# Biases, own features and residual sums: from TensorE and ScalarE to VectorE in a four-layer graph network kernel

## The chip, the cores and the metric

The kernel runs on one core of a Trainium2 chip. Its time is the device time of one execution in microseconds (us). The engines are named as the profile names them: PE (TensorE matmul), PEld (TensorE weight load), DVE (VectorE), ACT (ScalarE), POOL (GpSimd), SP (SyncE). They run their own queues of instructions side by side and wait for one another by semaphores. Line numbers such as L812 are those of the kernel before.

## What is computed

Sixteen graphs (batches) of 1024 nodes with 64 features each go through four layers, each followed by a layer norm of the sum of its input and its output. Layer 0 multiplies by the adjacency matrix and applies an MLP with tanh. Layer 1 is a mean over the neighbours, weighted by the adjacency. Layers 2 and 3 take, for each node and each feature, a weighted sum of three quantiles over the node's neighbours, after some edges are removed ("dilation"), add the node's own features, and apply an MLP with relu.

```python
def _L0(h, adjacency, W1, b1, W2, b2):
    messages = jnp.einsum('bij,bjh->bih', adjacency, h)
    node_in = jnp.concatenate([h, messages], axis=-1)
    return jnp.tanh(node_in @ W1 + b1) @ W2 + b2

def _L1(x, A):
    deg = jnp.clip(jnp.sum(A, axis=2, keepdims=True), 1.0, None)
    return jnp.matmul(A / deg, x)

def _L2(x, adj, mask, W1, b1, W2, b2):          # _L3 is the same in form
    adj_d = _dilate_adj(adj, mask)
    agg = _weighted_nanquantile_agg(x, adj_d > 0)   # quantiles 0.25, 0.5, 0.75
    out = (1.0 + EPS_GIN) * x + agg
    h = jax.nn.relu(jnp.einsum('bnc,ch->bnh', out, W1) + b1)
    y = jnp.einsum('bnh,ho->bno', h, W2) + b2
    return y * mask[..., None].astype(dtp)

x = _layernorm(x + _L0(x, adj, ...))
x = _layernorm(x + _L1(x, adj))
x = _layernorm(x + _L2(x, adj, nodemask, ...))
x = _layernorm(x + _L3(x, adj, nodemask, ...))
```

## The kernel before

The nodes of a graph are 8 tiles of 128 (NT = 8); two halves of four tiles (NH = 2, G = 4) are handled at a time. The nodes are sorted by the number of their neighbours, so that each tile has lists of one length. Seven tiles get their neighbours' features by indirect DMA (`got_s`), the eighth, with up to 33 slots, by matmuls with one-hot matrices: VectorE makes `hot` for a slot, TensorE picks the rows into `pgk`, ScalarE copies four slots at a time. VectorE then sorts the lists with networks of min and max.

The parts of all graphs are written as Python generators and woven together when the program is built. Each `yield n` says that the generator's next instructions are to be placed n us of VectorE work later in the source; the count is kept as VectorE's instructions are issued (`Metered`). A `yield` costs no time on the chip: it only sets the order of the instructions in each engine's queue. Round k sorts layer 2 of graph k and layer 3 of graph k - 2.

```python
    # features(b, e): layers 0 and 1 of a graph
        for h in range(NH):
            ...
            pd = s.psum.tile([P, G, C], F32, name="pd", tag="x", bufs=1)
            for q in range(G):
                nc.tensor.matmul(pd[:, q, :], hid_t[:, q * P : (q + 1) * P], w02s, start=True, stop=False)
                nc.tensor.matmul(pd[:, q, :], ones_row, bias_rows[0], start=False, stop=False)
                nc.tensor.matmul(pd[:, q, :], ident, x_s[:, h * G + q, :], start=False, stop=True)
            yield 10
            nc.scalar.copy(y[:, h * G : (h + 1) * G], pd)                       # L451
        yield 4
        yield from settle(x1[:, :, :C], y, "x")                                 # layer norm
        ...
            dve.tensor_scalar(deg[:, 0], pa[:, :, C], 1.0, None, op0=ALU.max)
            dve.reciprocal(deg[:, 1], deg[:, 0])
            yield 1
            for q in range(G):
                nc.scalar.activation(y[:, h * G + q, :], pa[:, q, :C], AF.Copy, scale=deg[:, 1, q : q + 1])  # L475

    # lists(b, e, pace): the neighbours' numbers and counts (cut)
            yield 2.6
        yield 3
        dve.tensor_scalar(own[:, :, 0], key[:, 4], 1.0, None, op0=ALU.add)
        ...
    # ordered(b, e, order, own): each entry's slot number (cut)
            for c in range(g, g + G):
                for c2 in range(c + 1):
                    nc.tensor.matmul(pp[:, c - g, :], steps[:, ONSET + (c - c2) * P :][:, :P], place[:, c2, :], ...)
            yield 9
            dve.tensor_mul(place[:, g : g + G, :], pp, place[:, g : g + G, :])

    # fill(k): the long tile's slots (cut)
            for i in range(1, size):
                ...
                hot = s.lists.tile([P, NT, P], BF, name="hot", bufs=HOTS)       # HOTS = 6
                dve.tensor_scalar(hot, e.place, float(i), None, op0=ALU.is_equal)
                ...
                pick(pg[:, i - first, :], hot, e.parts[m], whole)               # 24 matmuls
                yield 2.1

    # finish(b, e, layer, agg): own features, MLP, mask, layer norm
        for h in range(NH):
            pt = s.psum.tile([P, HALF], F32, name="pt", tag="m", bufs=1)
            for q in range(G):
                nc.tensor.matmul(pt[:C, q * P : (q + 1) * P], xc[:, h * G + q, :], ident, start=True, stop=False)
                nc.tensor.matmul(pt[:C, q * P : (q + 1) * P], agg[:, h * G + q, :], ident, start=False, stop=True)
            yield 7
            nc.scalar.copy(o_t, pt[:C])
            yield 3
            nc.tensor.matmul(ph[:H], w1s, o_t, start=True, stop=True)
            yield 7
            nc.scalar.activation(h_t, ph[:H], AF.Relu, bias=b1c)
            yield 3
            pd = s.psum.tile([P, G, C], F32, name="pd", tag="m", bufs=1)
            for q in range(G):
                nc.tensor.matmul(pd[:, q, :], h_t[:, q * P : (q + 1) * P], w2s, start=True, stop=False)
                nc.tensor.matmul(pd[:, q, :], ones_row, bias_rows[1 + layer], start=False, stop=True)
            yield 9
            for t in range(h * G, (h + 1) * G):
                nc.scalar.activation(y[:, t, :], pd[:, t - h * G, :], AF.Copy, scale=e.mask[:, t : t + 1])   # L812
        yield 4
        dve.tensor_add(y, y, xc)
        yield from settle(xn, y, "m")
```

Of the kernel before, what the change touches and what calls it, by code (L numbers as in the profile page):

```python
# [21 lines left out]
P = 128  # L22
# [190 lines left out]
def adj_resnorm_kernel(ctx: ExitStack, tc: tile.TileContext, x, adj_t, nodemask, w01, b01, w02, b02,  # L213
# [53 lines left out]
        nc.sync.dma_start(t, ap)  # L267
        return t

    def row(ap, name):  # L270
        return weight(ap.rearrange("(o c) -> o c", o=1), name)

    def column(ap, name):
        return weight(ap.rearrange("(c o) -> c o", o=1), name)

    w01s, b01c, w02s = weight(w01, "w01s"), column(b01, "b01c"), weight(w02, "w02s")
    mlps = [
        (weight(w21, "w21s"), column(b21, "b21c"), weight(w22, "w22s")),
        (weight(w31, "w31s"), column(b31, "b31c"), weight(w32, "w32s")),
    ]  # L280
    bias_rows = [row(b, f"bias_row{i}") for i, b in enumerate((b02, b22, b32))]
    ones_row = const.tile([1, P], F32, name="ones_row")
    nc.vector.memset(ones_row, 1.0)
    def hats(dst, pos_shape, n1, places):

        m = s.work.tile(pos_shape, F32, name="hat_m", tag=f"hat_m{pos_shape[-1]}", bufs=1)
# [116 lines left out]
    def features(b, e):  # L403

        x_s = s.feat.tile([P, NT, C], F32, name="x_s", bufs=1)
        load_x(b, x_s)
        adj = {}

        def load(i):

            if i < 2 * NT:
                adj[i] = s.feat.tile([P, NT, P], F32, name="adj_r", bufs=3)
                cols = slice(i % NT * P, i % NT * P + P)
                nc.sync.dma_start(adj[i], adj_t[entry(b), :, cols].rearrange("o (t p) i -> p (o t) i", p=P))

        load(0)
        load(1)
        x1 = s.feat.tile([P, NT, C + 1], F32, name="x1", bufs=1)
        y = s.work.tile([P, NT, C], F32, name="y_x", bufs=1)
        dve.memset(x1[:, :, C : C + 1], 1.0)  # L420
        yield 8
        for h in range(NH):

            node_in = s.work.tile([P, HALF], F32, name="node_in", bufs=1)
            px = s.psum.tile([P, HALF], F32, name="px", tag="x", bufs=1)
            for q in range(G):
# [12 lines left out]
            yield 3  # L439
            nc.tensor.matmul(px[:C], w01s, node_in, start=True, stop=True)  # L440
            yield 9
            hid_t = s.work.tile([C, HALF], F32, name="hid_t", tag="node_in", bufs=1)
            nc.scalar.activation(hid_t, px[:C], AF.Tanh, bias=b01c)
            yield 3
            pd = s.psum.tile([P, G, C], F32, name="pd", tag="x", bufs=1)
            for q in range(G):
                nc.tensor.matmul(pd[:, q, :], hid_t[:, q * P : (q + 1) * P], w02s, start=True, stop=False)
                nc.tensor.matmul(pd[:, q, :], ones_row, bias_rows[0], start=False, stop=False)
                nc.tensor.matmul(pd[:, q, :], ident, x_s[:, h * G + q, :], start=False, stop=True)
            yield 10  # L450
            nc.scalar.copy(y[:, h * G : (h + 1) * G], pd)  # L451
        yield 4
        yield from settle(x1[:, :, :C], y, "x")
        while b and not entries[b - 1].packed:
            yield 2
        near = s.sets.tile([P, NT, N], F16, name="near")
        for h in range(NH):
            pa = s.psum.tile([P, G, C + 1], F32, name="pa", tag="x", bufs=1)
            for q in range(G):
                i = NT + h * G + q  # L460
                t = i - NT
                rows = slice(t * P, (t + 1) * P)
                for jt in range(NT):
                    nc.tensor.matmul(pa[:, q, :], adj[i][:, jt, :], x1[:, jt, :], start=jt == 0, stop=jt == NT - 1)  # L464
                yield 4
                dve.tensor_scalar(near[:, :, rows], adj[i], 0.0, None, op0=ALU.is_gt)
                dve.tensor_mul(near[:, t, rows], near[:, t, rows], off_diag)
                load(i + 2)
            yield 8
            deg = s.work.tile([P, 2, G], F32, name="deg", bufs=1)  # L470
            dve.tensor_scalar(deg[:, 0], pa[:, :, C], 1.0, None, op0=ALU.max)
            dve.reciprocal(deg[:, 1], deg[:, 0])
            yield 1
            for q in range(G):
                nc.scalar.activation(y[:, h * G + q, :], pa[:, q, :C], AF.Copy, scale=deg[:, 1, q : q + 1])  # L475
        yield 5
        e.near = near
        x2 = s.feat.tile([P, NT, C], F32, name="x2", tag="x_s", bufs=1)
        dve.tensor_add(y, y, x1[:, :, :C])
        yield from settle(x2, y, "x")  # L480
        nc.sync.dma_start(table[0][b % 3][:N, :].rearrange("(t p) c -> p t c", p=P), x2)
        while b >= 2 and not entries[b - 2].filled[0]:
            yield 2
        parts = s.feat.tile([P, NT, 3, C], BF, name="x2p")
        yield from split(x2, parts, y)
        e.parts[0] = parts

    def lists(b, e, pace):
# [69 lines left out]
        for t in range(NT + 1):  # L558
# [12 lines left out]
                junk = s.work.tile([P, NT, P], F16, name="junk", tag="dist", bufs=3)  # L571
                nc.scalar.activation(junk, left(t - 1), AF.Sign, accum_out=key[:, 4, t - 1 : t])
            yield 2.6
        yield 3


        dve.tensor_scalar(own[:, :, 0], key[:, 4], 1.0, None, op0=ALU.add)
# [57 lines left out]
    def ordered(b, e, order, own):  # L635
# [41 lines left out]
        for g in reversed(range(0, NT, G)):  # L677
            pp = s.psum.tile([P, G, P], F32, name="pp", tag="s", bufs=1)
            for c in range(g, g + G):
                for c2 in range(c + 1):  # L680
                    nc.tensor.matmul(pp[:, c - g, :], steps[:, ONSET + (c - c2) * P :][:, :P], place[:, c2, :],
                                     start=c2 == 0, stop=c2 == c)
            yield 9
            dve.tensor_mul(place[:, g : g + G, :], pp, place[:, g : g + G, :])
            yield 3
        e.place = place
# [43 lines left out]
    def fill(k):  # L730
# [6 lines left out]
        for m, b, e in members(k):  # L737
# [8 lines left out]
            for i in range(1, size):  # L746
# [6 lines left out]
                    nc.tensor.matmul(pg[:, i - first, :], e.none,  # L753
                                     ident_b[: KW - 1, i - 1 : i].to_broadcast([KW - 1, C]), start=True, stop=False)
                pick(pg[:, i - first, :], hot, e.parts[m], whole)
                yield 2.1
                if i % 4 == 2 and waiting:
                    empty()
                if i % 4 == 0:
# [26 lines left out]
    def finish(b, e, layer, agg):  # L786

        xc = e.xs[layer]
        w1s, b1c, w2s = mlps[layer]
        y = s.work.tile([P, NT, C], F32, name="y_m", bufs=1)  # L790
        for h in range(NH):
            pt = s.psum.tile([P, HALF], F32, name="pt", tag="m", bufs=1)
            for q in range(G):
                nc.tensor.matmul(pt[:C, q * P : (q + 1) * P], xc[:, h * G + q, :], ident, start=True, stop=False)
                nc.tensor.matmul(pt[:C, q * P : (q + 1) * P], agg[:, h * G + q, :], ident, start=False, stop=True)
            yield 7
            o_t = s.work.tile([C, HALF], F32, name="o_t", bufs=1)
            nc.scalar.copy(o_t, pt[:C])
# [6 lines left out]
            yield 3  # L805
            pd = s.psum.tile([P, G, C], F32, name="pd", tag="m", bufs=1)
            for q in range(G):
                nc.tensor.matmul(pd[:, q, :], h_t[:, q * P : (q + 1) * P], w2s, start=True, stop=False)
                nc.tensor.matmul(pd[:, q, :], ones_row, bias_rows[1 + layer], start=False, stop=True)
            yield 9  # L810
            for t in range(h * G, (h + 1) * G):
                nc.scalar.activation(y[:, t, :], pd[:, t - h * G, :], AF.Copy, scale=e.mask[:, t : t + 1])  # L812
        yield 4
        dve.tensor_add(y, y, xc)
        xn = agg if layer else s.feat.tile([P, NT, C], F32, name="x3s", bufs=3)
        yield from settle(xn, y, "m")
# [175 lines left out]
        nc.vector.reciprocal(st[:, 0], st[:, 3])  # L992
        nc.vector.tensor_mul(dst, y, st[:, 0, :, None].to_broadcast([P, NT, C]))

    def per_row(ap):
        t = s.work.tile([P, C], F32, name="per_row")
        nc.sync.dma_start(t, ap.rearrange("(o c) -> o c", o=1).to_broadcast([P, C]))
        return t

    def transposed(src, name):  # L1000

        dst = s.work.tile([C, N], F32, name=name, bufs=1)
# [7 lines left out]
    def layer0(adj_half, x_s, x1):  # L1010
# [18 lines left out]
            nc.tensor.matmul(pd[:, t, :], hid_t[:, t * P : (t + 1) * P], w02s, start=True, stop=True)  # L1029
        y = s.work.tile([P, NT, C], F32, name="y")  # L1030
        nc.vector.tensor_add(y, pd, x_s)
        nc.vector.tensor_add(y, y, per_row(b02)[:, None, :].to_broadcast([P, NT, C]))
        nc.vector.memset(x1[:, :, C : C + 1], 1.0)
        layernorm(x1[:, :, :C], y)

# [15 lines left out]
        nc.vector.tensor_add(y, y, x1[:, :, :C])  # L1051
        layernorm(x2, y)

    def mlp(xc, agg, mask, layer, dst):
        w1s, b1c, w2s = mlps[layer]
        y = s.work.tile([P, NT, C], F32, name="y")
        nc.vector.tensor_add(agg, agg, xc)
        o_t = transposed(agg, "x_t")
# [9 lines left out]
        nc.vector.tensor_add(y, pd, per_row((b22, b32)[layer])[:, None, :].to_broadcast([P, NT, C]))  # L1068
# [131 lines left out]
    with tc.If(nc.values_load(over_d[:, B:]) > 0):  # L1200
        with tc.For_i(0, B) as b:
            with tc.If(nc.values_load(over_d[:, ds(b, 1)]) > 0), ExitStack() as general:
# [32 lines left out]
                for layer, (xc, xn) in enumerate(((x2, x3), (x3, x1[:, :, :C]))):  # L1235
                    with tc.tile_pool(name=f"g_lists{layer}", bufs=1) as lists:
                        long_quantiles(lists, table[layer][0], idx, wts, agg)
                    with tc.tile_pool(name=f"g_dense{layer}", bufs=1) as dense:
                        dense_quantiles(dense, xc, valid, count, longest, agg)
                    mlp(xc, agg, mask, layer, xn)  # L1240
# [34 lines left out]
```

## Time and profile before

| | |
|---|---|
| time, median of 3 runs | 5381.86 us (5374.81 to 5388.84) |
| span of the profiled execution | 5376.9 us |
| mean granted TensorE clock | 0.765 of full speed |
| sixteen graphs, rounds | 18 rounds, some 316 us each in the steady part |

The page gives each engine's busy time as a share of the span, and the same in 40 slices as tenths. A wait is put down to the instruction that ended it. VectorE's instructions all stand at one line, L207 (the helper that counts them), so they are told apart by the tiles that they write and read. The largest groups that the change touches or has beside it are these (count, busy us, mean ns of one):

| engine | what | count | busy us | mean ns |
|---|---|---|---|---|
| PE | picks of the long tile, pgk<-x2p,hot and pgk<-x3p,hot | 24576 | 971.8 | 201 to 204 |
| PE | MLP bias, pd<-bias_row,ones_row (L809) | 512 | 133.0 | 347 |
| PE | features bias (L448) and own features (L449) | 512 | 142.3 | 363 and 375 |
| PE | transpose with sum, pt (L794 and L795) | 1024 | 253.4 | 333 to 348 |
| DVE | hot<-place 128x1024 | 1024 | 436.5 | 437 |
| ACT | mask, y_m<-pd,mask_s (L812) | 256 | 59.1 | 320 |
| ACT | degree scaling, y_x<-pa,deg (L475) | 128 | 29.3 | 309 |
| ACT | copy y_x<-pd (L451) | 32 | 12.0 | 376 |

### The profile page before, as it was taken

What the parts mean: (1) busy time and instruction counts of PE and PEld (TensorE: products, weight loads), DVE (VectorE), ACT (ScalarE), POOL (GpSimd) and SP (SyncE); (2) the same over time, 40 slices, a digit from 0 to 9 for tenths busy, and PEclk for the clock granted to TensorE, in tenths of its full rate; (3) what the DMA queues carried; (4) which work ended last, traced back from release to release, by engine and by line L of the source; (5) the groups of instructions that cost most, each with busy time, mean ns of one, the idle gap of its engine ahead of it and who ended that gap; (6) DMA issues with size and microseconds to landing.
All of it is one profiled execution on the core that took longest, in us unless ns stands there. A gap on an engine that the chain in (4) does not pass through costs nothing. (4 is left out here: it accounts for less than half of the span.)

```text
span 5376.9 us, 112554 instructions
## 1 busy us (share of the span) xinstructions
PE 3746.3 (70%) x45268; PEld 2875.6 (53%) x45304; DVE 4444.1 (83%) x8819; ACT 2296.3 (43%) x6214; POOL 3659.3 (68%) x3228
## 2 busy tenths in 40 slices
PE   6888876595967769595876849688694966434452
PEld 5656655374746657363655636466473745433341
DVE  2487777989898898979889797988979789977975
ACT  3364462455445363634445353443535344222222
POOL 0335575878777777867768686776868577777662
PEclk7887787696878779787877868687797877666655
DMA  2222321222222212112221221222122121111010
GB/s 82 64 60 54 79 49 50 50 51 61 53 60 54 58 48 65 41 35 59 56 56 46 48 52 42 60 55 54 41 56 53 40 46 24 25 23 25 19 24 10
DMA packets 420186, 259.37 MB, mean 48 GB/s; under 512 B 106164, under 2 KB 368452, under 8 KB 419652
## 3 DMA queue, kind: packets, MB, share of 16 engines
q0 software_dynamic: 102400, 105.06, 10.1%
q1 hardware_dynamic: 317252, 147.02, 9.8%
q8 instruction: 356, 5.83, 0.5%
q14 instruction: 178, 1.46, 0.1%
HBM read 239.27 MB, written 12.58 MB: 47 GB/s over the span
## 5 line engine op out<-in xcount | busy, mean ns | idle before, releaser
L359 POOL DMA_INDIRECT got_s<-table,idx x2944 | 3355.2, 1140 | 1473.6 <-issue 686.4
L355 PEld LDWEIGHTS <-hot 128*128 128x128 bf16 x24576 | 881.8, 104 | 611.8 <-DVE hot L207 468.2
L522 PE MATMUL pr<-steps,near 128*128 128x512 bf16 x1500 | 435.1, 453 | 378.0 <-ACT nb_st L503 223.8
L355 PE MATMUL pgk<-x3p,hot 128*128 128x64 bf16 x12288 | 493.2, 204 | 229.0 <-DVE hot L207 203.0
L355 PE MATMUL pgk<-x2p,hot 128*128 128x64 bf16 x12288 | 478.6, 201 | 239.1 <-DVE hot L207 216.1
L744 ACT COPY got<-pgk 128x256 f32<-128x256 f32 x256 | 94.5, 369 | 1186.0 <-PE pgk L355 1175.5
L207 DVE TENSOR_TENSOR other<-got_s 128x512 f32<-128x512 f32 (+8 forms) x900 | 514.8, 584 | 90.3 <-DMA got_s<-table,idx 75.5
L207 DVE TENSOR_SCALAR hot<-place 128x1024 bf16<-128x1024 f16 x1024 | 436.5, 437 | 129.8 <-PE pgk L355 127.2
L522 PEld LDWEIGHTS <-near 128*128 128x128 f16 x1536 | 171.2, 112 | 634.8 <-issue 521.1
L207 DVE TENSOR_TENSOR got_s<-got_s 128x384 f32<-128x384 f32 (+7 forms) x918 | 490.7, 537 | 17.5
L774 ACT ACTIVATE got_s<-got_s,wts 128x64 f32<-128x64 f32 x1568 | 400.2, 338 | 221.6 <-DVE got_s L207 221.0
L609 PE MATMUL pk<-near,order 128*128 128x512 f16 x2048 | 485.2, 393 | 0.0
L464 PE MATMUL pa<-x,adj_r 128*128 128x65 f32 x2048 | 355.2, 349 | 93.4 <-DMA adj_r<-in_adj_dram 39.2
L566 PE MATMUL pv<-minus_n,takes 128*128 128x128 bf16 x1024 | 224.7, 249 | 279.0 <-DVE takes L207 278.4
L207 DVE TENSOR_TENSOR got_s<-other 128x512 f32<-128x512 f32 (+8 forms) x774 | 409.2, 541 | 8.1
L464 PEld LDWEIGHTS pa<-x,adj_r 128*128 128x128 f32 x2048 | 343.4, 264 | 107.6 <-DMA adj_r<-in_adj_dram 40.5
L566 PEld LDWEIGHTS <-takes 128*128 128x128 bf16 x1024 | 112.9, 110 | 416.7 <-DVE takes L207 318.1
L207 DVE TENSOR_TENSOR other<-other 128x128 f32<-128x128 f32 (+13 forms) x558 | 318.6, 571 | 15.1
L609 PEld LDWEIGHTS <-order 128*128 128x128 bf16 x2048 | 198.5, 101 | 242.9 <-issue 42.5
L565 PE MATMUL pv<-scaled,near 128*128 128x128 f16 x1024 | 226.2, 250 | 105.0 <-ACT near L570 93.8
L528 ACT ACTIVATE junk<-pr,nb_st 128x1024 f16<-128x1024 f32 x256 | 282.1, 1107 | 28.7 <-PE pr L522 28.6
L431 PE MATMUL px<-adj_r,x_s 128*64 128x128 f32 x2048 | 274.7, 293 | 2.1 <-ACT node_in L434 1.4
(204 smaller groups left out, 7486.6 us busy)
## 6 DMA issues: line engine op xcount, KB each, us to landing
adj_r<-in_adj_dram SPq DMA_DIRECT2D x256, 512.0 KB
got_s<-table,idx POOLq DMA_INDIRECT x2944
x_s<-in_x_dram SPq DMA_DIRECT2D x16, 256.0 KB
table<-x SPq DMA_DIRECT2D x16, 256.0 KB
x<-table SPq DMA_DIRECT2D x16, 256.0 KB
table<-x3s,rows POOLq DMA_INDIRECT x128
out_dram<-agg,out_rows POOLq DMA_INDIRECT x128
table<-no_row SPq DMA_DIRECT2D x6, 0.2 KB
```

Of the source, the lines that this page charges most:

```text
L207: return call(*args, **kwargs)
L355: nc.tensor.matmul(dst, hot[:, c, :], parts[:, c, q, :], start=first and c + q == 0, stop=c == NT - 1 and q == 2)
L359: nc.gpsimd.indirect_dma_start(out=dst, out_offset=None, in_=tab, in_offset=bass.IndirectOffsetOnAxis(ap=rows, axis=0))
L431: nc.tensor.matmul(px[C:, q * P : (q + 1) * P], x_s[:, jt, :], adj[t][:, jt, :], start=jt == 0, stop=jt == NT - 1)
L464: nc.tensor.matmul(pa[:, q, :], adj[i][:, jt, :], x1[:, jt, :], start=jt == 0, stop=jt == NT - 1)
L522: nc.tensor.matmul(pr[:, h * HALF : (h + 1) * HALF], near[:, c, t * P : (t + 1) * P], steps[:, ONSET + h * HALF - c * P :][:, :HALF], star ...
L528: nc.scalar.activation(junk, prs[t - 1], AF.Sign, bias=lim[:, i, t - 1 : t], scale=-1.0, accum_out=cut_at[:, i, t - 1 : t])
L565: nc.tensor.matmul(pv[:, cols], near[:, c, rows], scaled[:, c, :], start=True, stop=False)
L566: nc.tensor.matmul(pv[:, cols], takes[:, c, rows], minus_n, start=False, stop=False)
L609: nc.tensor.matmul(cols, order[:, c, t * P : (t + 1) * P], left(c, slice(h * G, (h + 1) * G)), start=c == 0, stop=c == NT - 1)
L744: nc.scalar.copy(got[:, m, waiting[0] : waiting[0] + 4, :], waiting[1])
L774: nc.scalar.activation(prods[:, m, i, :], got[:, m, slot_id, :], AF.Copy, scale=e.wts[:, t, i : i + 1])
```

## The change

The change takes three kinds of addition out of TensorE's accumulation in PSUM, and two scalings out of ScalarE, and gives all of them to VectorE. The bias rows are loaded once, spread over the 128 partitions. It is to relieve TensorE and ScalarE, and to let VectorE read PSUM without another engine between. It also changes three distances in the source: the long tile's slots (2.1 to 2.4), the product that makes the slot numbers (`place`, 9 to 12), and the read-out of the counts (3 to 6).

```diff
-    def row(ap, name):
-        return weight(ap.rearrange("(o c) -> o c", o=1), name)
+    def per_row(ap, name):
+        t = const.tile([P, C], F32, name=name)
+        nc.sync.dma_start(t, ap.rearrange("(o c) -> o c", o=1).to_broadcast([P, C]))
+        return t
 ... (the weights of the layers now hold b02r, b22r, b32r; ones_row and bias_rows are gone)
@@ features
-                nc.tensor.matmul(pd[:, q, :], hid_t[:, q * P : (q + 1) * P], w02s, start=True, stop=False)
-                nc.tensor.matmul(pd[:, q, :], ones_row, bias_rows[0], start=False, stop=False)
-                nc.tensor.matmul(pd[:, q, :], ident, x_s[:, h * G + q, :], start=False, stop=True)
+                nc.tensor.matmul(pd[:, q, :], hid_t[:, q * P : (q + 1) * P], w02s, start=True, stop=True)
             yield 10
-            nc.scalar.copy(y[:, h * G : (h + 1) * G], pd)
-        yield 4
+            dve.tensor_add(y[:, h * G : (h + 1) * G], pd, x_s[:, h * G : (h + 1) * G])
+        dve.tensor_add(y, y, b02r[:, None, :].to_broadcast([P, NT, C]))
 ...
-            yield 1
-            for q in range(G):
-                nc.scalar.activation(y[:, h * G + q, :], pa[:, q, :C], AF.Copy, scale=deg[:, 1, q : q + 1])
-        yield 5
+            dve.tensor_mul(y[:, h * G : (h + 1) * G], pa[:, :, :C], deg[:, 1, :, None].to_broadcast([P, G, C]))
@@ lists
-        yield 3
+        yield 6
@@ ordered
-            yield 9
+            yield 12
             dve.tensor_mul(place[:, g : g + G, :], pp, place[:, g : g + G, :])
@@ fill
-                yield 2.1
+                yield 2.4
@@ finish
+        dve.tensor_add(agg, agg, xc)
+        yield 2
 ...
-                nc.tensor.matmul(pt[:C, q * P : (q + 1) * P], xc[:, h * G + q, :], ident, start=True, stop=False)
-                nc.tensor.matmul(pt[:C, q * P : (q + 1) * P], agg[:, h * G + q, :], ident, start=False, stop=True)
+                nc.tensor.transpose(pt[:C, q * P : (q + 1) * P], agg[:, h * G + q, :], ident)
 ...
-                nc.tensor.matmul(pd[:, q, :], h_t[:, q * P : (q + 1) * P], w2s, start=True, stop=False)
-                nc.tensor.matmul(pd[:, q, :], ones_row, bias_rows[1 + layer], start=False, stop=True)
+                nc.tensor.matmul(pd[:, q, :], h_t[:, q * P : (q + 1) * P], w2s, start=True, stop=True)
             yield 9
-            for t in range(h * G, (h + 1) * G):
-                nc.scalar.activation(y[:, t, :], pd[:, t - h * G, :], AF.Copy, scale=e.mask[:, t : t + 1])
-        yield 4
+            dve.tensor_add(y[:, h * G : (h + 1) * G], pd, b2r[:, None, :].to_broadcast([P, G, C]))
+        dve.tensor_mul(y, y, e.mask[:, :, None].to_broadcast([P, NT, C]))
         dve.tensor_add(y, y, xc)
```

What is cut away from the diff is in a path for graphs with longer lists, which these inputs do not take.

More of the change, by code (lines that the diff above doesn't have):

```diff
@@ L268, in weight @@
         return t
-    def row(ap, name):
-        return weight(ap.rearrange("(o c) -> o c", o=1), name)
+    def per_row(ap, name):
+        t = const.tile([P, C], F32, name=name)
+        nc.sync.dma_start(t, ap.rearrange("(o c) -> o c", o=1).to_broadcast([P, C]))
+        return t
     def column(ap, name):
         return weight(ap.rearrange("(c o) -> c o", o=1), name)
-    w01s, b01c, w02s = weight(w01, "w01s"), column(b01, "b01c"), weight(w02, "w02s")
+    w01s, b01c, w02s, b02r = weight(w01, "w01s"), column(b01, "b01c"), weight(w02, "w02s"), per_row(b02, "b02r")
     mlps = [
-        (weight(w21, "w21s"), column(b21, "b21c"), weight(w22, "w22s")),
-        (weight(w31, "w31s"), column(b31, "b31c"), weight(w32, "w32s")),
-    ]
-    bias_rows = [row(b, f"bias_row{i}") for i, b in enumerate((b02, b22, b32))]
-    ones_row = const.tile([1, P], F32, name="ones_row")
-    nc.vector.memset(ones_row, 1.0)
+        (weight(w21, "w21s"), column(b21, "b21c"), weight(w22, "w22s"), per_row(b22, "b22r")),
+        (weight(w31, "w31s"), column(b31, "b31c"), weight(w32, "w32s"), per_row(b32, "b32r")),
+    ]
     def hats(dst, pos_shape, n1, places):
@@ L788, in finish @@
         xc = e.xs[layer]
-        w1s, b1c, w2s = mlps[layer]
+        w1s, b1c, w2s, b2r = mlps[layer]
         y = s.work.tile([P, NT, C], F32, name="y_m", bufs=1)
+        dve.tensor_add(agg, agg, xc)
+        yield 2
         for h in range(NH):
@@ L993, in layernorm @@
         nc.vector.tensor_mul(dst, y, st[:, 0, :, None].to_broadcast([P, NT, C]))
[L995 to L998, printed above, removed]
     def transposed(src, name):
@@ L1031, in layer0 @@
         nc.vector.tensor_add(y, pd, x_s)
-        nc.vector.tensor_add(y, y, per_row(b02)[:, None, :].to_broadcast([P, NT, C]))
+        nc.vector.tensor_add(y, y, b02r[:, None, :].to_broadcast([P, NT, C]))
         nc.vector.memset(x1[:, :, C : C + 1], 1.0)
@@ L1052, in layer1, with mlp @@
         layernorm(x2, y)
-    def mlp(xc, agg, mask, layer, dst):
-        w1s, b1c, w2s = mlps[layer]
+    def mlp(xc, agg, mask, weights, dst):
+        w1s, b1c, w2s, b2r = weights
         y = s.work.tile([P, NT, C], F32, name="y")
@@ L1067, in mlp @@
             nc.tensor.matmul(pd[:, t, :], h_t[:, t * P : (t + 1) * P], w2s, start=True, stop=True)
-        nc.vector.tensor_add(y, pd, per_row((b22, b32)[layer])[:, None, :].to_broadcast([P, NT, C]))
+        nc.vector.tensor_add(y, pd, b2r[:, None, :].to_broadcast([P, NT, C]))
         nc.vector.tensor_mul(y, y, mask[:, :, None].to_broadcast([P, NT, C]))
@@ L1239, in adj_resnorm_kernel @@
                         dense_quantiles(dense, xc, valid, count, longest, agg)
-                    mlp(xc, agg, mask, layer, xn)
+                    mlp(xc, agg, mask, mlps[layer], xn)
                     if layer == 0:
```

## The prediction

> **What bounds the kernel now.** I read the page's first part, then the 40 slices, then what VectorE (DVE) waits for, and last one round of the loop in windows and in the timeline. First the busy times:
>
> ```profile
> PE 3746.3 (70%) x45268; PEld 2875.6 (53%) x45304; DVE 4444.1 (83%) x8819; ACT 2296.3 (43%) x6214; POOL 3659.3 (68%) x3228
> ...
> DVE  2487777989898898979889797988979789977975
> ```
>
> VectorE is the fullest engine, and from the seventh slice on it is at 70 to 90%. The span of 5376.9 us less 4444.1 us busy leaves 933 us. Its waits account for most of that (columns: who waited for whom, total us, times, longest us):
>
> ```profile
> DVE hot L207 <- PE pgk L355: 127.2, 58, 6.9
> DVE y_m L207 <- ACT y_m L812: 115.7, 13, 20.3
> DVE other L207 <- DMA got_s<-table,idx: 75.5, 10, 19.2
> DVE place L207 <- PE pp L681: 75.3, 15, 9.3
> DVE near L207 <- DMA adj_r<-in_adj_dram: 65.5, 14, 9.9
> DVE ln_st_x L207 <- ACT y_x L451: 63.1, 9, 44.9
> DVE own L207 <- ACT junk L572: 55.3, 11, 22.6
> ```
>
> The reader should see that four of these seven (hot, y_m, place, own: 373 us) name exactly the places that the change touches. They are not spread evenly. One steady round, 2290 to 2607 us, in windows (us, then busy us of PE, weight load, DVE, ACT, POOL, then granted TensorE clock, DMA share, GB/s):
>
> ```profile
> 2290.00:2330.00 40.00, 37.89 (x435) 29.61 (x432) 33.46 (x71) 16.63 (x43) 32.02 (x27) 0.76 0.22 49
> 2330.00:2370.00 40.00, 39.54 (x541) 26.52 (x539) 21.68 (x40) 9.48 (x25) 21.61 (x23) 0.95 0.19 46
> ...
> 2450.00:2490.00 40.00, 21.32 (x173) 16.61 (x173) 38.21 (x84) 19.88 (x78) 31.16 (x30) 0.67 0.30 77
> 2490.00:2530.00 40.00, 22.98 (x84) 9.02 (x84) 39.21 (x64) 25.23 (x61) 32.99 (x24) 0.80 0.19 32
> ```
>
> A round has two halves. At 2290 to 2370 TensorE is full (77 of 80 us) and VectorE idles 25 us; at 2450 to 2530 VectorE is full (77 of 80) and TensorE is half empty. So VectorE sets the pace in one half and TensorE in the other. In the TensorE half I looked at one VectorE stall in the timeline, first ACT, then DVE:
>
> ```profile
> 2360.43 0.37 ACT L744 COPY got<-pgk 128x256 f32<-128x256 f32 x1 [14.05 <-PE pgk L355]
> 2360.70 1.02 ACT L620 CAST code<-pk 128x1024 f16<-128x1024 f32 x1
> 2361.60 0.94 ACT L812 ACTIVATE y_m<-pd,mask_s 128x64 f32<-128x64 f32 x4
> ```
> ```profile
> 2362.58 0.69 DVE L207 TENSOR_TENSOR y_m<-y_m,x2s 128x512 f32<-128x512 f32 x1 [10.89 <-ACT y_m L812]
> ```
>
> VectorE stood 10.89 us for four ScalarE instructions of 0.94 us together. They stood behind a copy of the long tile's slots, which itself waited for TensorE. Their own operand, pd, was complete at about 2350.4, when the last bias matmul had run. The wait is thus one of queue order, not of work.
>
> **What the Trainium skill says.** (1) "PSUM — Partial Sum Buffer", section "Engine vs sequencer instructions": the queues of ScalarE, VectorE and GpSimd are strictly first in, first out, and matmuls keep their order. The stall above agrees: 10.89 us behind a copy that has nothing to do with it. (2) "VectorE: DVE Perf Modes", section "The perf-mode tier table (the rule you actually need)": a tensor_tensor in fp32 runs at the basic rate whether its operands lie in SBUF or PSUM. The trace agrees: the 128x512 product place<-pp, whose one operand is in PSUM, takes 684 ns, the same shape in SBUF 687 to 692 ns. So I take SBUF rows for the new PSUM additions. (3) "Perfetto Trace Analysis", section "Optimization Strategy": a kernel can have regimes with different contended engines, and interleaving them can help. The windows agree that there are two regimes here; the change shifts load from the one engine to the other in both.
>
> **The change part by part.**
>
> *TensorE, removed.* The records count two per fp32 matmul. Bias rows in the MLP: 512 records (133.0 us busy); bias in features: 256 (70.0); own features through the identity in features: 256 (72.3); one of the two matmuls per transposed block in the MLP: 512 (about 129.5, the mean of 340 to 348 ns). That is 404.8 us of busy time, but records overlap. From start to start, eight MLP bias records beside eight others filled 2290.12 to 2293.00, so 1.45 us for the eight; a features group of 24 records filled 2378.13 to 2382.59, 4.46 us, of which 16 go: 3.0 us. At a lower clock, at 2294 to 2301, the same group took 7.2 us, and 16 are 4.9. Per round: two features groups 7.9; four MLP bias groups 5.8; four half transposes (each half of 2305.35 to 2308.04) 5.4: 19.1 us, times 16 about 306 us of TensorE's sequence. Of it some 12 us lie between 2285 and 2385, in the TensorE half and just after (two features groups, two MLP groups, one transpose group).
>
> *ScalarE, removed.* 256 masks of 128x64 (59.1 us), 128 degree scalings (29.3), 32 copies (12.0): 100 us of 2296, and with them that many hops in a queue that blocks.
>
> *VectorE, added.* For 128x512 I use 0.687 us, for 128x256 0.421 us (rows got_s<-other and got_s<-got_s,other). MLP, 32 times: one sum with own features 0.687, two additions from PSUM 0.842, one mask product 0.687: 2.216, together 70.9. Features, 16 times: two additions from PSUM 0.842 and a bias addition 0.687: 24.5. Degree scaling, 16 times two: 13.5. Sum 108.9 us, 6.8 a round, 2.0% of the span. Nothing is taken off VectorE, and in the VectorE half it is paid in full.
>
> *Spacing.* The kernel interleaves its generators by a count of VectorE time; the yields set how far apart instructions stand in the queues. Slots of the long tile 2.4 apart instead of 2.1 make 64 slots take 154 instead of 134 of these units. In the round before, the slots end at 2432 and the tail's sort starts at 2488, so there is room for 20 us. Between 2290 and 2370 about 33 slots become 29; a slot of 24 matmuls at the fast clock is 0.7 to 0.9 us, so another 3 us of TensorE leave the crowded half. The product place stands 3 units later, and the count read-out 3 units later.
>
> **What comes back.** VectorE's stalls over the whole run, my estimates from the waits above. y_m: VectorE will wait for pd itself, not for ScalarE's queue; in the stall shown pd was ready 12 us before, so I give back two thirds, 76 of 116. place: 15 waits, each up to 3 us shorter by spacing, but the first TensorE excess also falls: 30 of 75. hot: the excess of TensorE falls by 15 us a round against stalls of 12, but the new additions are new stopping points, twice in features and twice in each MLP, only 9 or 10 units behind their matmuls, while six hot buffers allowed some 13; I count 102 given back and 65 newly lost at pd, net 37. own: 10 of 55; ln_st_x: 8 of 63, since most of that is the start. Sum 161. But a stall removed in TensorE's half can reappear at the next thing TensorE makes (code, pk, near), because the queue behind has the same work in it; I let 65 of it reappear. Net 96.
>
> 5381.9 + 108.9 - 96 = 5394.8; I write 5395.
>
> **The rivals.** *A: VectorE is the bound and the sum is paid.* All 108.9 us come on top, new PSUM waits eat what TensorE gives: about 5490. For it: 83% busy, 98% in the second half of a round, and VectorE's own reads of pd rise from none to six per batch. Against it: 36 us of named idle per round in the TensorE half. *B: TensorE's half shortens by what is removed from it.* 12 + 3 us less in each of some 14 rounds, 210 us, less the part of VectorE's 6.8 us that falls in its own half (about 4 a round, 60): 5382 - 150, about 5230. For it: TensorE 77 of 80 us there. Against it: VectorE gets work in that half too, and ScalarE's waits for pgk (1175.5 us) still order that queue. *C: gathers.* If VectorE sped up, POOL's 2944 gathers of 1140 ns would be next: 230 of 317 us a round, so they have room; only the last two or three rounds, where other<-got_s waits 75 us for DMA, are held by them, and nothing changes there.
>
> **Range and chances.** A sets the upper and B the lower end, neither likely in full: 5305 to 5485. Faster by over 2% means under 5274, which needs B nearly whole: 0.07. Slower by over 2% means above 5490, which needs A whole: 0.08. Within 2%: 0.85.
>
> **What would show it.** In the profile after: DVE busy near 4553, PE near 3340, ACT near 2196. Waits of y_m: on pd of PE, below 50 us, none on ScalarE. hot below 100, place near 45, new waits of y_x and y_m on pd near 65 together. In the VectorE half nothing but the added time. I am wrong if idle of VectorE falls by far more than 96 us (then TensorE's half was a true bound and rival B holds) or hardly falls (rival A); a different order of the interleaved generators, which shifts transfers of adj_r or gathers into the way, would be a third cause.

## The result and the profile after

The changed kernel takes 5245.43 us (median of 4 runs, 5240.36 to 5252.46) against 5383.99 us of the kernel before: ratio 0.9746, 95% interval 0.9728 to 0.9763. It is 2.5% faster, and below the range of the prediction.

First the busy times and VectorE's slices in the page of the changed kernel:

```profile
PE 3384.9 (65%) x43512; PEld 2580.3 (49%) x43512; DVE 4554.6 (87%) x9026; ACT 2206.1 (42%) x5792; POOL 3759.9 (72%) x3228
...
DVE  2578888989899998999999999999999999877976
```

VectorE does 110.5 us more (4554.6 less 4444.1), and the span is 138 us shorter. So VectorE's idle fell from 932.8 to 684.0 us, by 249 us. Its slices in the middle stand at 9 nearly everywhere, where before 7 and 8 were mixed in. What VectorE waits for in the changed kernel (columns as before):

```profile
DVE other L207 <- DMA got_s<-table,idx: 110.7, 17, 21.9
DVE best L207 <- ACT code L614: 98.1, 25, 9.4
DVE y_x L207 <- PE pd L446: 48.9, 6, 19.5
DVE y_m L207 <- PE pd L803: 45.2, 10, 7.6
DVE own L207 <- ACT junk L566: 29.6, 2, 23.0
DVE near L207 <- DMA adj_r<-in_adj_dram: 25.9, 8, 11.8
DVE hot L207 <- PE pgk L354: 23.0, 23, 4.4
...
DVE place L207 <- PE pp L675: 11.4, 7, 2.5
```

The reader should see three things. The wait of hot fell by 104 us and that of place by 64. y_m no longer waits for ScalarE; it and y_x wait for pd of TensorE. And part of the idle came back elsewhere: best, which needs code (copied by ScalarE from TensorE's pk), went from 45 to 98 us, the gathers from 76 to 111.

Part of one round of the changed kernel, in windows of 40 us (us, busy us of PE, weight load, DVE, ACT, POOL, then clock, DMA share, GB/s):

```profile
2267.00:2307.00 40.00, 39.01 (x588) 27.47 (x586) 32.39 (x57) 11.80 (x29) 30.70 (x31) 1.00 0.32 79
2307.00:2347.00 40.00, 31.75 (x576) 25.02 (x572) 39.17 (x72) 18.13 (x55) 31.31 (x29) 0.91 0.14 26
```

There were two windows in which TensorE was full and VectorE at 22 to 33 us of 40. One is left, and VectorE has 32 of 40 us there. From one end of the long tile's sort to the next, a steady round takes 296 to 308 us; before it took 312 to 324 from 2267 us on, and 298 to 310 in the four rounds ahead of that. Of a steady round VectorE was busy 279 us (before 272) and idle 17 to 29 (before 39 to 52 from 2267 us on).

### The profile page after: what moved, and what is told of

Read it like the earlier page. It is cut to its first block, busy times and chain, and to the rows that moved or that the text cites. A ratio compares the mean times of both kernels' runs of the same rounds, so it can differ in the third digit from the quotient of the medians.

```text
span 5238.6 us, 108870 instructions
## 1 busy us (share of the span) xinstructions
PE 3384.9 (65%) x43512; PEld 2580.3 (49%) x43512; DVE 4554.6 (87%) x9026; ACT 2206.1 (42%) x5792; POOL 3759.9 (72%) x3228
## 5 line engine op out<-in xcount | busy, mean ns | idle before, releaser
L358 POOL DMA_INDIRECT got_s<-table,idx x2944 | 3433.5, 1166 | 1282.6 <-issue 657.7
L354 PEld LDWEIGHTS <-hot 128*128 128x128 bf16 x24576 | 942.9, 108 | 857.9 <-DVE hot L207 726.6
L354 PE MATMUL pgk<-x3p,hot 128*128 128x64 bf16 x12288 | 562.6, 214 | 366.4 <-DVE hot L207 349.8
L207 DVE TENSOR_TENSOR got_s<-got_s 128x256 f32<-128x256 f32 (+7 forms) x918 | 490.8, 537 | 19.2
L560 PE MATMUL pv<-minus_n,takes 128*128 128x128 bf16 x1024 | 238.3, 259 | 305.9 <-DVE takes L207 304.9
L559 PE MATMUL pv<-scaled,near 128*128 128x128 f16 x1024 | 239.9, 260 | 214.7 <-ACT near L564 214.6
L461 PE MATMUL pa<-x,adj_r 128*128 128x65 f32 x2048 | 333.7, 334 | 48.9 <-DMA adj_r<-in_adj_dram 27.6
L461 PEld LDWEIGHTS pa<-x,adj_r 128*128 128x128 f32 x2048 | 322.6, 249 | 54.5 <-DMA adj_r<-in_adj_dram 28.2
```

The lines of the kernel that those rows point to most:

```text
L207: return call(*args, **kwargs)
L354: nc.tensor.matmul(dst, hot[:, c, :], parts[:, c, q, :], start=first and c + q == 0, stop=c == NT - 1 and q == 2)
L358: nc.gpsimd.indirect_dma_start(out=dst, out_offset=None, in_=tab, in_offset=bass.IndirectOffsetOnAxis(ap=rows, axis=0))
L559: nc.tensor.matmul(pv[:, cols], near[:, c, rows], scaled[:, c, :], start=True, stop=False)
L560: nc.tensor.matmul(pv[:, cols], takes[:, c, rows], minus_n, start=False, stop=False)
```

## The experiments

Three theories were set against one another. *TensorE*: what counts is the work taken out of the half of a round that TensorE fills. *Queue*: what counts is that VectorE no longer stands behind ScalarE's queue for y_m. *Spacing*: the wider distances in the source do it alone.

### The change taken apart

These runs share a chip on which the kernel before took 5392.78 us.

`m1_ops_old_spacing` is the change without its distances:

```diff
-                yield 2.4      # long tile's slots
+                yield 2.1
-            yield 12           # place
+            yield 9
-        yield 6                # counts
+        yield 3
```

> The change with the three old distances (2.1, 9, 3), for a chip where the kernel before takes about 5380 us. TensorE theory: the work moved is most of the gain, the spacing a small part: 5255 to 5300 us, hot waits 35 to 75 us. Spacing theory: about 5490.

Measured 5280.93 us, ratio 0.9788 (0.9769 to 0.9807). The moved work without the three distances gives 2.1%, in spite of its VectorE cost, where the spacing theory had a loss (5490 us). So the distances are not needed for most of the gain. Its waits:

```profile
DVE hot L207 <- PE pgk L354: 65.2, 48, 4.0
DVE y_m L207 <- PE pd L803: 52.5, 17, 6.7
DVE place L207 <- PE pp L675: 51.1, 15, 4.4
DVE y_x L207 <- PE pd L446: 44.6, 5, 19.7
```

VectorE's idle here is 738 us (span 5288.9, busy 4550.6), 194 less than in the kernel before. The small yields that stood around the removed ScalarE instructions (4, 1 and 5, and a new 2) are part of what is called moved work here and in all that follows, and so is what ScalarE is spared.

`m2_spacing_only` is the kernel before with only the distances of the change:

```diff
-                yield 2.1      # long tile's slots
+                yield 2.4
-            yield 9            # place
+            yield 12
-        yield 3                # counts
+        yield 6
```

> The kernel before with the three new distances alone. TensorE theory: 3 us a round leave the crowded half, 5320 to 5360 us; hot and place waits fall, y_m on ScalarE stays. Spacing theory: 5140 to 5180.

Measured 5191.45 us, ratio 0.9632 (0.9615 to 0.9648). This is faster than the changed kernel. The TensorE theory, which counted 3 us a round for the distances, missed it by 129 us or more; it is 11 us above the range of the spacing theory. No instruction was added or removed. VectorE's waits in this kernel:

```profile
DVE other L207 <- DMA got_s<-table,idx: 223.6, 20, 19.2
DVE y_m L207 <- ACT y_m L812: 55.6, 13, 20.3
DVE ln_st_x L207 <- ACT y_x L451: 50.1, 3, 45.4
...
DVE hot L207 <- PE pgk L355: 24.9, 13, 8.9
DVE best L207 <- ACT code L620: 18.4, 12, 6.0
...
DVE place L207 <- PE pp L681: 1.1, 1, 1.1
```

hot fell from 127 to 25 us and place from 75 to 1, with TensorE's work as before. y_m halved, though ScalarE's instructions still stand between. In ten steady rounds, between 1400 and 4300 us, its single wait fell from 6.3 to 10.9 us in the kernel before to 1.3 to 1.8 in m2; most of the 55.6 us left are three waits in the last rounds. The stall that the prediction showed looks like this in m2, first ACT, then DVE:

```profile
2299.06 0.37 ACT L744 COPY got<-pgk 128x256 f32<-128x256 f32 x1 [8.33 <-PE pgk L355]
2299.33 0.94 ACT L812 ACTIVATE y_m<-pd,mask_s 128x64 f32<-128x64 f32 x4
2300.30 0.73 DVE L207 TENSOR_TENSOR y_m<-y_m,x2s 128x512 f32<-128x512 f32 x1 [1.27 <-ACT y_m L812]
```

The mask still stands behind a copy that waits for TensorE, and its operand was complete 4.8 us before. So the order of the queue is the same, and it costs little where TensorE is less late.

What leads the list now are the gathers, at 224 us: a stall of 10 to 18 us in each of twelve rounds from 1150 to 4400 us, where the kernel before had none. The same 200 us of a round (from the first slot of the long tile on), first in the kernel before, then in m2 (columns as above):

```profile
2268.00:2468.00 200.00, 179.94 (x2517) 143.30 (x2519) 156.62 (x320) 69.79 (x201) 131.25 (x118) 0.86 0.23 54
2234.00:2434.00 200.00, 189.35 (x2665) 156.94 (x2666) 182.93 (x371) 97.21 (x268) 157.02 (x142) 0.87 0.28 66
```

In m2 both engines are nearly full: TensorE 189 us, VectorE 183, against 180 and 157. The traces also show how. From the first to the last hot of a round, the 64 slots last 161 to 169 us in the steady rounds of the kernel before (from 2268 us on), though the yields place them over only 134 us of VectorE work; in the round shown, 31 us of stalls for TensorE, or behind ScalarE's queue, make up the rest. In m2 they are placed over 154 us of work and last 165 to 173 us. So the stretch is hardly longer; VectorE work now fills what had been stalls. In m1, with less TensorE work and 134 us again, it lasts 147 to 149 us. That the stall is what TensorE needs for the stretch less the VectorE work placed beside it is my reading of these lengths. The three distances were changed together; which of them does most was not tried.

`m3_zero_matmuls` is the change with TensorE's old load put back. The added matmuls add zeros into the same sums:

```diff
                 nc.tensor.matmul(pd[:, q, :], hid_t[...], w02s, start=True, stop=False)
+                nc.tensor.matmul(pd[:, q, :], ident[:1], zeros[:1], start=False, stop=False)
+                nc.tensor.matmul(pd[:, q, :], ident, zeros, start=False, stop=True)
 ... (the same for the MLP's bias; one with zeros for each transposed block)
```

> The change with TensorE's old load put back as zero-adding matmuls. TensorE theory: 12 to 14 us a round come back on top of 5245, and the 109 us on VectorE stay: 5420 to 5480 us. Queue and spacing theories: 5245 to 5265.

Measured 5452.59 us, ratio 1.0117 (1.0100 to 1.0134). TensorE's load, with everything else of the change in place, costs 207 us over the changed kernel. Its waits:

```profile
DVE best L207 <- ACT code L618: 148.1, 27, 14.0
DVE y_m L207 <- PE pd L809: 122.5, 24, 11.9
DVE y_x L207 <- PE pd L450: 104.8, 19, 24.6
```

Set beside m2, this run has as many matmuls and the same three distances, and yet it takes 261 us more. Of these 118 are VectorE's busy time (4561.8 and 4443.3), and the rest, 144, is idle. VectorE now reads pd itself, 10 or 9 units behind the matmuls, and stands when TensorE is late: 227 us at y_m and y_x, where m2 waits 106 us for y_m and ln_st_x, behind ScalarE. best stands 148 us (m2: 18), and the gathers 143 us less than in m2. How much of the idle is due to the direct reads, and how much to other instructions having moved, was not separated.

So the 2.5% can be read as a sum of three, in us, as m2 against before, m3 against m2, changed kernel against m3: the distances -201, the additions read and made by VectorE (with ScalarE's relief in it) +261, the load off TensorE -207. That is -147; the pair itself differs by 139, as the kernel before was 9 us faster in its set. The order matters, since the distances and the relief remove the same stalls: alone -201 and (with VectorE's cost in it) -112, together no more than -139. VectorE's idle says it more plainly: 188 us less with the distances alone, 194 less with the moved work alone, 249 less with both.

### The same with TensorE roomy

In these four runs two of the three matmuls of every pick are left out (the two lower parts of the split features, so that the output is less exact). TensorE has 18432 fewer of its 45304 weight loads in the kernel before, and the rest is unchanged. The kernel before in full took 5378.99 us on this chip.

```diff
-            for q in range(3):
-                nc.tensor.matmul(dst, hot[:, c, :], parts[:, c, q, :], ...)
+            nc.tensor.matmul(dst, hot[:, c, :], parts[:, c, 0, :], start=first and c == 0, stop=c == NT - 1)
```

> The kernel before with one of three matmuls left in every pick (the two lower parts of the split features are left out, so the output is less exact): 18432 of 45304 weight loads fewer on TensorE, everything else the same. TensorE theory: stalls of VectorE on hot nearly vanish and the time falls clearly below the kernel before: where that takes 5380 us, 5180 to 5260; where TensorE idles for issue (7150 us), below 6000. Queue theory: y_m still waits over 100 us on ScalarE and the time falls by under 60 us.

Measured 5198.41 us, ratio 0.9664 (0.9644 to 0.9683). The picks left out were worth 181 us to the kernel before, within the TensorE theory's range; y_m's wait on ScalarE fell to 65 us with it. But hot, which was to nearly vanish, still waits 66 us. VectorE's idle is 733 us (span 5177.5, busy 4444.5): a third way to give TensorE room, and nearly the same idle as in m1 (738) and m2 (745).

`h2_after_light`: the same cut in the changed kernel.

> The changed kernel with the same picks left out, to be set beside the run before it. TensorE theory: with TensorE roomy the change has nothing to relieve, so its 109 us on VectorE show: slower than the light kernel before by 20 to 110 us where that runs near 5200; where TensorE still idles for issue, a gain of under 1%. Queue and spacing theories: the same gain as without the cut, 2.5%, about 130 us.

Measured 5223.41 us, 0.9706 (0.9690 to 0.9722) of the full kernel before. Here the change is a loss: 25 us more than h1. Taking the picks away gives the changed kernel only 22 us (5245 to 5223). Its two largest waits are for transfers and no longer for TensorE:

```profile
DVE other L207 <- DMA got_s<-table,idx: 163.4, 24, 21.7
DVE near L207 <- DMA adj_r<-in_adj_dram: 76.4, 18, 13.4
```

The light kernel with the distances alone was not run, so these 25 us are of the whole change and not of the moved work.

`h3_after_light_mask_twice`: h2 with VectorE's mask product of the MLP made twice; with a mask of 0 and 1 the result is the same.

```diff
         dve.tensor_mul(y, y, e.mask[:, :, None].to_broadcast([P, NT, C]))
+        dve.tensor_mul(y, y, e.mask[:, :, None].to_broadcast([P, NT, C]))
```

> The changed kernel with the same picks left out and the mask product done twice (22 us more on VectorE). If VectorE sets the pace once TensorE has room: 15 to 25 us more than the light changed kernel. If something else does: under 8 us.

Measured 5247.32 us, 24 us over h2 for 32 more products of 0.692 us in its trace, 22 us. VectorE's added work is paid in full here.

`h4_after_light_zeros`: h2 with the zero matmuls of m3.

> The changed kernel with the same picks left out and TensorE's old additions put back as matmuls that add zeros. TensorE theory: with room on TensorE they cost less than in the full kernel (there 1.06 of the changed kernel with old distances): under 2% more than the light changed kernel.

Measured 5309.58 us, 86 us over h2 (1.65%), where the same matmuls cost 207 us in the full kernel. The same load on TensorE costs less than half where TensorE has room; its own length doesn't give its price.

### A version that follows the account by halves

`k1_split_by_half` puts pieces back where their old engine seemed to have room: layer 3's MLP and the degree scaling as before, and the features' bias as a 65th row of a matmul that is there anyway.

```diff
+        if layer == 0:
             dve.tensor_add(agg, agg, xc)
 ... (layer 2: transpose, bias and mask as in the change; layer 3: as in the kernel before)
-            dve.tensor_mul(y[:, h * G : (h + 1) * G], pa[:, :, :C], deg[...])
+            for q in range(G):
+                nc.scalar.activation(y[:, h * G + q, :], pa[:, q, :C], AF.Copy, scale=deg[:, 1, q : q + 1])
-                nc.tensor.matmul(pd[:, q, :], hid_t[...], w02s, start=True, stop=True)
+                nc.tensor.matmul(pd[:, q, :], hid_t[...], w02e, start=True, stop=True)   # row 65: tanh(20), bias
-        dve.tensor_add(y, y, b02r[:, None, :].to_broadcast([P, NT, C]))
```

> A version that puts each piece where its engine has room: the MLP of layer 2 as in the change, the MLP of layer 3 (which falls in the half of the round that VectorE fills) as in the kernel before, the degree scaling back on ScalarE, the features' bias as a 65th row of the matmul that is there anyway. VectorE loses 35 + 13.5 + 11 = 60 us of work. TensorE theory with VectorE setting the pace elsewhere: 5190 to 5215 us, 0.6 to 1.1% under the change. If the roomy half is not roomy: no better than 5245.

Measured 5267.17 us, ratio 0.9762 (0.9742 to 0.9782), no better than the change. VectorE's busy time fell by 68 us, and its idle rose by 95, above all at two places:

```profile
DVE y_m L207 <- PE pd L821: 111.0, 12, 10.6
DVE counted L207 <- PE pn L701: 84.1, 12, 15.0
```

They were 45 and 21 us in the changed kernel. The gain that was expected (5190 to 5215 us) failed; what the expectation said for a roomy half that is not roomy, no better than 5245, came true. Whether the half lacks room or the yields, with less VectorE work between them, placed the work worse was not separated. A count of work by halves didn't say where the queues meet.

### Sets in which TensorE was starved

In three earlier sets the kernel before took 7137 to 7240 us. The trace of e2, the kernel before with only the new distances, shows why (columns: who, for what, total us, times, longest us):

```profile
PE pgk L355 <- issue: 593.1, 761, 3.3
PE ordered_x L355 <- issue: 313.7, 310, 2.6
```

"issue" is time in which TensorE waited for nothing that the profile shows; in the recorded pair these two lines are missing. Why TensorE's instructions came late was not settled; one of the chips was also that of m1 to m3, so it isn't the chip alone. These runs stand for another balance of the engines, and I don't use them for the 2.5%.

`e1_ops_old_spacing` and `f1_ops_old_spacing` are the kernel of m1, `e2_spacing_only` and `f2_spacing_only` that of m2, `e3_zero_matmuls` and `f3_zero_matmuls` that of m3, each in two sets.

> The change with the three old distances (2.1, 9, 3). TensorE theory (what counts is the work taken out of TensorE's crowded half): most of the gain stays, 5260 to 5300 us, hot waits of VectorE at 40 to 70 us. Spacing theory (the wider distances alone make the gain): the 109 us of VectorE are paid with nothing in return, about 5490. Queue theory (VectorE no longer stands behind ScalarE's queue): about 5300, y_m waits as in the changed kernel, below 60 us, but place still near 75.

> The change with the three old distances, again, since in the first set even the kernel before took 7136 us on that chip, with TensorE idle for issue. Ratio to the kernel before where that takes some 5380 us. TensorE theory: most of the gain stays, 0.978 to 0.987. Spacing theory: 1.02. Queue theory: about 0.985.

> The kernel before with the three new distances (2.4, 12, 6) and nothing else. Spacing theory: the idle that vanished (249 us) vanishes here too and no VectorE work is added, so 5140 to 5180 us. TensorE theory: spacing takes some 3 us a round out of the crowded half, 5330 to 5360. Queue theory: about 5380, y_m still waits some 115 us on ScalarE.

> The kernel before with the three new distances alone, again. Spacing theory: 0.955 to 0.963 (idle goes, no VectorE work is added). TensorE theory: 0.990 to 0.996. Queue theory: 1.000, y_m still waits on ScalarE.

> The change with TensorE's old load put back as matmuls that add zeros into the same sums (same results, VectorE and ScalarE as in the changed kernel). TensorE theory: the crowded half takes back 10 to 14 us in each of 16 rounds, 5400 to 5450 us. Queue and spacing theories: within 20 us of the changed kernel's 5245.

> The change with TensorE's old load put back as matmuls that add zeros, again. TensorE theory: 1.003 to 1.013 of the kernel before (5400 to 5450 us where that takes 5380). Queue and spacing theories: 0.975 to 0.978, as the change.

`e4_mask_on_dve` and `f4_mask_on_dve` are the kernel before with only ScalarE's mask taken over:

```diff
-            for t in range(h * G, (h + 1) * G):
-                nc.scalar.activation(y[:, t, :], pd[:, t - h * G, :], AF.Copy, scale=e.mask[:, t : t + 1])
+            dve.tensor_mul(y[:, h * G : (h + 1) * G], pd, e.mask[:, h * G : (h + 1) * G, None].to_broadcast([P, G, C]))
```

> The kernel before, but the mask product of the MLP done by VectorE from PSUM (64 products of 128x256, 27 us) instead of 256 ScalarE instructions; TensorE's work and all distances unchanged. Queue theory: y_m waits fall from 116 to below 50 us, the time to about 5310 to 5340. TensorE theory: the stall moves on to what TensorE makes next, 5370 to 5400. Spacing theory: 27 us are paid, about 5410.

> The kernel before with the MLP's mask product on VectorE from PSUM, again. Queue theory: 0.987 to 0.992 with y_m waits below 50 us. TensorE theory: 0.998 to 1.004, since the stall moves to what TensorE makes next.

`g1_after_again` is the changed kernel, `g2_mask_twice` the same with the second mask product of h3.

> The changed kernel itself, on whatever chip this is. If the kernel before takes about 5380 us here, the change takes about 5245 (0.975). If TensorE idles for issue here as in the first two sets (before above 7000 us), TensorE sets more of the pace and the TensorE theory expects a larger gain, 0.95 to 0.965; the queue and spacing theories expect no larger one, 0.97 to 0.98.

> The changed kernel with the MLP's mask product done twice on VectorE (32 more products of 128x512, 22 us; the result is the same, the mask being 0 or 1). Where before takes 5380: if VectorE now sets the pace nearly everywhere, the full 22 us on top of 5245, 5262 to 5272; if TensorE does, under 8 us. Where TensorE idles for issue: under 10 us on top of the changed kernel there.

| kernel | ratio to before, with interval |
|---|---|
| moved work, old distances (e1, f1) | 0.9615 (0.9557 to 0.9673), 0.9584 (0.9543 to 0.9626) |
| distances only (e2, f2) | 0.9887 (0.9828 to 0.9946), 0.9954 (0.9940 to 0.9968) |
| zero matmuls (e3, f3) | 1.0192 (1.0124 to 1.0259), 1.0177 (1.0136 to 1.0218) |
| mask on VectorE (e4, f4) | 1.0148 (1.0086 to 1.0210), 1.0017 (0.9984 to 1.0050) |
| the change (g1), with the mask twice (g2) | 0.9888 (0.9795 to 0.9981), 0.9904 (0.9888 to 0.9919) |

Where TensorE is starved, relief is worth 4% and spreading alone almost nothing. Both together, the change itself, gain only 1.1%: there the wider distances cost some 3% on top of the relief, read across sets (g1 beside e1 and f1). None of the theories' ranges (0.95 to 0.965, and 0.97 to 0.98) holds g1's 0.9888, and the cause stays open. g1 has only two executions, so what the second mask product costs in g2 is not clear. Taking the mask off ScalarE gained nothing in either run. It was not tried where TensorE wasn't starved, so of the queue theory m2 is the test: it nearly removes y_m's wait in the steady rounds with the hop in place. That the hop costs nothing where TensorE is late is not shown.

## Why the prediction was wrong

*What is added and removed.* Right. VectorE was to gain 108.9 us and gained 110.5; PE was to show 3340 us of busy time and shows 3385, ACT 2196 and 2206. That fp32 additions from PSUM cost what they cost in SBUF held, as the Trainium skill has it ("VectorE: DVE Perf Modes", "The perf-mode tier table (the rule you actually need)"): the 128x256 additions y_m<-pd and y_x<-pd take 415 to 418 ns in the changed kernel, rows of that shape in SBUF 418 to 427.

*Two regimes in a round.* Right, and the gain hangs on it: the change gains 2.5% in the full kernel and loses 0.5% where TensorE is roomy (h2 beside h1).

*What comes back.* This step failed. I let 161 us of stalls come back and 65 reappear, net 96; VectorE's idle fell by 249. The largest term is what VectorE waits for pd. I gave back two thirds of y_m's wait (40 us left), left 55 of ln_st_x's 63, and then charged 65 us of new waits at pd on top: 160 us in all for the places that hang on pd. Measured are 94 (45 at y_m, 49 at y_x), since the new waits mostly took the place of the old ones, and the relief itself makes pd earlier: with TensorE's old load they are 227 (m3), without it 97 (m1) or 94. The others, in us given back: hot 104 (102 before that charge, so right), place 64 instead of 30, own 26 instead of 10, near 40 and key_c 18, which I hadn't counted. What reappeared, at best and the gathers, was 88 (53 and 35) instead of 65.

*Spacing.* Part of the same step, and the surprise lies in what it does alone. I took it as four slots fewer in the crowded half, "another 3 us of TensorE" a round. By itself it takes 188 us of idle away and 201 us of time (m2). But it doesn't explain the miss: the moved work without it already takes away 194 us of idle (m1, 5281 us, below my range), and inside the change the distances add only the 0.4% between the ratios of m1 and the change. The two cure the same stalls, some 31 us of a round in TensorE's half, so their effects don't add; I had priced each as a small share of these stalls. My count of slots was off as well: between 2290 and 2370 the trace has 24 hot and 19 slots of picks, not 33. And the stalls in TensorE's half of that round are 31 us, not the 36 that I held against rival A.

*The stall shown.* I read the 10.89 us at y_m as "one of queue order, not of work". The record is as read, but the conclusion was too narrow: ScalarE's queue stood because TensorE was late. With TensorE's work spread, the same order of the queue costs 1.27 us at this place (m2).

*The rivals.* B, whose 5230 us lies nearest, was right that TensorE's half gives back nearly what is lost there; I gave it too little weight because I let VectorE's new reads take most of it. These reads stand long when TensorE is loaded (227 us, m3), and less than half of that once it is relieved (94). A, the sum simply paid, comes out only where TensorE is roomy, and there at 25 us of 109. C was right about what comes next: in m2 and h2 the gathers lead the list with 224 and 163 us. But they don't have the room that I saw, and don't hold the last rounds alone: in m2 they stop VectorE in every steady round.

The best version found is m2, the kernel before with the three wider distances: 5191.45 us, 0.9632 of the kernel before, with nothing moved. Where TensorE is starved it is not the best: there the moved work with the old distances is (e1, f1).

## What to carry to other kernels

When two engines take turns as the bound within a round, first try to spread the crowded engine's work by its place in the program, before moving work to the other engine: here it took no instruction and gave 3.7%, against 2.5%. Two cures of the same stall don't add (188 and 194 us of idle apart, 249 together), so run each alone before you credit either. Neither the length of what is removed nor its share of busy time sizes the gain; price both sides, by adding harmless work to each engine in turn. And when an engine is to read an accumulator itself, look at how late the producer is: the same reads stood 227 us with TensorE loaded and 94 with it relieved.

## What the runs showed that was not expected

The same program took 5379 to 5393 us in some sets and 7137 to 7240 us in others. TensorE's picks, which follow each other at 29 to 54 ns in the recorded trace, came there in short groups with idle between that is put down to issue (906.8 us for the two groups shown, in e2). VectorE's busy time hardly differed (4453.6 us in e2, 4443.3 us in m2, the same kernel). A ratio measured under the one balance did not hold under the other: the distances alone gave 3.7% in the one and 0.5 to 1.1% in the other.
